# Linear attention and a sorted mixture of experts on one core: GpSimd's work beside the first block's sums of keys, five filler matmuls, and the order of the end

## The chip, the core and the metric

The kernel runs on one core of a Trainium2 chip. Its time is device time in microseconds (us) of the whole program. Five engines are named here: TensorE (PE in the profile, PEld its weight loads), VectorE (DVE), ScalarE (ACT), GpSimd (POOL) and SyncE (SP). SP only issues transfers in this kernel. ScalarE and GpSimd have DMA queues of their own. An engine executes its instructions in the order in which the program gives them. DMA transfers run beside the engines once they are issued.

## The reference, cut to what matters

The input x has 4 sequences of 2048 tokens, each of 256 numbers, all in float32. Two pre-norm layers follow each other:

```python
x = x + linear_attention(layernorm(x))     # 16 heads of 16, causal
x = x + moe(layernorm(x))                  # 8 experts, the best 2 of each token

# linear attention, per head, token after token
q, k = elu(q) + 1, elu(k) + 1
s = s + outer(k_i, v_i);  z = z + k_i
values = (q_i @ s) / (q_i . z + 1e-6);  out = values @ Wo + bo

# moe: logits over 8 experts, top 2, softmax of the two, the rest is zero
hmid = gelu(x @ w1[e] + b1[e])             # 256 -> 512
y    = hmid @ w2[e] + b2[e]                # 512 -> 256
out  = sum over the two chosen experts of weight * y
```

Two sums matter below: `z`, the running sum of keys, and the product of q and z, by which the result is divided.

## The kernel before, in words

**Attention in 16 blocks.** The 8192 tokens are cut into 16 blocks of 512. A block passes through three stages, and stage a of block s, stage b of block s−1 and stage c of block s−2 are emitted interleaved, step by step. A scheduler then orders each engine's instructions by their dependencies; SP alone keeps the order in which the program was written (`manual_schedule`, L108). `follow` (L161) forces one instruction behind another on an engine without a wait; `after` (L313) makes an instruction wait for others.

*Entering a block* (L227): VectorE takes the layernorm's statistics (L179, L182), a root is made, `xn` is written by VectorE and ScalarE (L218, L213), and GpSimd adds the output bias `bo` to x in place (L232, 128x1024), since x is used again only in stage c. For blocks up to 5 the root is one GpSimd operation, a power (L187); for later ones it is 11 small VectorE operations of Newton's method (L191 to L201).

*Stage a* (L383): TensorE transposes `xn` (pt_xn, L335) and multiplies it by Wk and Wq (pp, L402). elu+1 is two ScalarE operations (L341, L342) and one of VectorE (L343). VectorE scans k along the tokens (L412, one scan for each half of the channels, called m) and multiplies z by q in one operation of 128x1024 (L418). TensorE computes v (pv, L427), to which VectorE adds its bias (L431), and transposes k (pk, L446). Then pd (L458) sums q·z by head, VectorE adds epsilon (L464) and takes the reciprocal (L465), pr (L473) spreads it over the channels again, and VectorE divides q (L478).

*Stage b* (L487): scores (sc, L508), the causal mask (L513), the state (state_ps, L548, held in a PSUM bank of its own, then S, L559) and the values (pn, L530 and L537).

*Stage c* (L585): px multiplies the values by Wo (L597) and also gives the router's logits. VectorE adds x (L601) and the logits (L602). The sum x1 goes to `out` on ScalarE's queue (L603). VectorE picks the best two experts (L617 to L629), does the second layernorm (L632), writes the weights, token number and expert into four extra columns of the row `xn2` (L638 to L648), and, with two matmuls pc (L654, L657) that count the tokens before each one, finds each token's slot in its expert's list (L660 to L678). GpSimd then scatters the block's rows to the DRAM buffer `rows` in 8 indirect DMAs (L682).

**Experts in tiles of 256 rows.** After blocks 3, 4, 6, 8, 10, 12, 14 and 16 a `plan` (L696, VectorE) gives out a round of tiles: 5, 4, 8, 8, 8, 8, 8 and 22, so that tile 49 is the first of the last round. 68 tiles are always done and 3 more only if needed. A tile j passes through three parts:

- *turned* (L834): its rows are transposed (pt_xs, L840), copied (xT, L841), and their targets and weights taken (L847 to L853)
- *hidden* (L860): 16 matmuls with w1 (ph, L868), and gelu on ScalarE (L874)
- *output* (L879): 16 matmuls with w2 (py, L885), bias and weight on VectorE (y, L890, L894), then two scatters on GpSimd that add to `out` (L899)

TensorE's order is ph of j, pt_xs of j+1, py of j−1. SP issues, in this order for each j: rows of tile j+3 (L807), w1 of j+2 (L819), w2 of j+1 (L827), b2 of j+1 (L831). A load of rows waits for every row scatter that was emitted before it (L811). While attention is still under way, tiles are emitted between its steps; the lines after L982 share them out, and HOLD (L948) leaves five tiles to be emitted beside the last block's stage c or behind it. The last block is number 15. After it only tiles remain.

Of the kernel before, what the change touches and what calls it, by code (L numbers as in the profile page):

```python
# [16 lines left out]
P = 128  # L17
HEADS = 16
HD = 16
# [5 lines left out]
def kernel(  # L25
# [131 lines left out]

    def ins_of(i):
        return getattr(i, "ins", i)

    def follow(inst, other):  # L161

        tc.add_manual_dep(
            ins_of(inst), ins_of(other).name,
            mybir.DependencyInfo(
                mybir.DependencyClass.NoSync, mybir.DependencyReason.SCHED_ONLY
            ), reason="order of issue",
        )
# [3 lines left out]
    def layernorm(src, dst, root_of=None, power=False, behind=None, first=False):  # L172
# [11 lines left out]
        nc.vector.tensor_scalar_add(rstd, mv[:, :, 1], LN_EPS)  # L184
# [41 lines left out]

    def enter(n: int):  # L227
        xt = xs.pop(n)
        xn = att.tile([P, NT, D], F32, tag="xn", bufs=2, name=f"xn_{n}")
        std = small.tile([P, NT], F32, tag="std", bufs=3, name=f"std_{n}")  # L230
        layernorm(xt, xn, std, n <= QUIET, turn if n <= QUIET else None, n == 0)
        nc.gpsimd.tensor_tensor(  # L232
            xt, xt, bo_bc.unsqueeze(1).to_broadcast([P, NT, D]), ALU.add
        )
        entered[n] = xt, xn, std
# [52 lines left out]
    state_ps = ps_s.tile([P, NCC, 2, HD], F32, tag="state", name="state_ps")  # L288
# [17 lines left out]
    AFTER = mybir.DependencyInfo(mybir.DependencyClass.Sync, mybir.DependencyReason.DATA)  # L306
# [5 lines left out]

    def after(inst, others):  # L313
        for o in others:
            tc.add_manual_dep(inst, o.name, AFTER, reason="rows written before")

# [66 lines left out]
    def stage_a(n: int):  # L383
# [34 lines left out]
        i = nc.vector.tensor_tensor(z, z, qT, ALU.mult)  # L418
        if n > 0:
            turn[:] = [i]  # L420
        vp = vpads[n % 2]
# [20 lines left out]
        for t2 in range(NT // 2):  # L442
            pk = bank([P, 2, D], "pk")
            for j in range(2):
                for m in range(NCC):
                    nc.tensor.transpose(  # L446
                        pk[:, j, ts(m, P)], kT[:, m, ts(2 * t2 + j, P)], ident
                    )
            nc.scalar.copy(k_tok[:, 2 * t2 : 2 * t2 + 2, :], pk)
        if n < QUIET:  # L450

            enter(n + 1)
# [3 lines left out]
        for m in range(NCC):  # L456
            for t in range(NT):
                nc.tensor.matmul(  # L458
                    pd[W * t : W * t + W, :], heads[:, m, :], z[:, m, ts(t, P)],
                    start=(m == 0), stop=(m == NCC - 1), skip_group_check=True,  # L460
                    tile_position=(0, W * t),
                )
        rden = small.tile([P, P], F32, tag="rden", name="rden")
# [121 lines left out]
    def stage_c(n: int):  # L585
# [30 lines left out]
        for r in range(2):  # L616
            top = small.tile([P, NT], F32, tag=f"top{r}", name="top")  # L617
            nc.vector.tensor_reduce(top, lg, AX.X, ALU.max)
            eq = small.tile([P, NT, E], F32, tag=f"eq{r}", name="eq")
            nc.vector.tensor_tensor(eq, lg, wide(top), ALU.is_equal)  # L620
            nc.vector.tensor_tensor(eq, eq, prio_b, ALU.mult)
            first = small.tile([P, NT], F32, tag=f"first{r}", name="first")
            nc.vector.tensor_reduce(first, eq, AX.X, ALU.max)
            nc.vector.tensor_tensor(sel[:, :, r, :], eq, wide(first), ALU.is_equal)
            if r == 0:
                nc.vector.scalar_tensor_tensor(
                    lg, sel[:, :, 0, :], -3.0e38, lg, ALU.mult, ALU.add
                )
            tops.append(top)  # L629
        yield  # L630
        xn2 = att.tile([P, NT, R], F32, tag="xn2", bufs=3, name=f"xn2_{n}")
        rstd = layernorm(x1, xn2[:, :, 0:D])  # L632
# [9 lines left out]
        nc.vector.tensor_scalar_add(xn2[:, :, D], token, float(n * TB))  # L642
# [11 lines left out]
        nc.tensor.matmul(  # L654
            pc[:, 0].rearrange("p m e -> p (m e)"), before, sel_f, start=True, stop=True
        )
        nc.tensor.matmul(  # L657
# [132 lines left out]
    plans = {}  # L790

    def slot_tiles(todo):
# [4 lines left out]
        def fetch_rows(j):  # L797
# [13 lines left out]
            after(i, writes + cleared)  # L811
# [48 lines left out]
        def hidden(j):  # L860
            xT, w1t, bias = (state[j][key] for key in ("xs", "w1", "bias"))
            hT = moe.tile([P, NFC, ST], F32, tag="hT", name="hT")
            for f2 in range(NFC // 2):
                ph = bank([P, 2, ST], "ph")
                for i in range(2):
                    f = 2 * f2 + i
                    for cc in range(NCC):
                        nc.tensor.matmul(  # L868
                            ph[:, i, :], w1t[:, cc, ts(f, P)], xT[:, cc, :],
                            start=(cc == 0), stop=(cc == NCC - 1),  # L870
                        )
# [7 lines left out]
        def output(j):  # L879
# [3 lines left out]
            for a in range(NS):  # L883
                for f in range(NFC):
                    nc.tensor.matmul(  # L885
# [10 lines left out]
            def store():  # L896
                mine = []
                for a in range(NS):
# [4 lines left out]
                    ))  # L903

# [20 lines left out]
        for j in range(J + 1):  # L925
# [4 lines left out]
            if j + LEAD < J:  # L930
                fetch_rows(j + LEAD)
# [4 lines left out]
            if j > 0:  # L936
                wait.append(output(j - 1))
            while len(wait) > (j < J):
                wait.pop(0)()
            if j + 1 < J:  # L940
                fetch_out(j + 1)
            if j < J:
# [5 lines left out]
    HOLD = 5  # L948
# [24 lines left out]
    for s in range(NBLK + 2):  # L973
# [18 lines left out]
        while gens:  # L992
            for it in list(gens):
# [3 lines left out]
                while ran < share and ran * order < i * share:  # L997
# [7 lines left out]
    while work.step():  # L1005
        pass
    in_order.close()
    held = nc.values_load(holding[0][0:1, 0:1], min_val=0, max_val=ROUNDS[-1])
# [49 lines left out]
```

## Time and profile before

| | |
|---|---|
| median of 3 runs | 1089.88 us (1088.99 to 1090.7) |
| profiled execution | 1089.58 us, of which the span is 1087.9 us |
| mean granted TensorE clock | 0.972 |
| TensorE busy, 0 to 35 us | 21.83 of 35 us |
| TensorE busy, 300 to 700 us | 394.97 of 400 us |
| TensorE busy, 850 to 890 us | 28.72 of 40 us, clock 0.87 |
| TensorE busy, 890 to 1060 us | 170.00 of 170 us, DMA 0.91 busy, 233 GB/s |
| last matmul ends | 1074.89 us |
| GpSimd's bias adds (L232) | 16, from 2.34 to 2.95 us each |
| row loads, issue to landing (median) | 4.1 us |
| w1 and w2 loads, issue to landing (median) | 5.3 us |
| GpSimd's row scatters, issue to landing (median) | 2.5 us |

How to read it: the span runs from the first to the last instruction of one profiled execution; the time of a run has some 1.7 us around it. "Busy" is the time in which at least one instruction of an engine runs. The clock is the share of TensorE's full speed that the chip granted it. In a timeline a row is: start in us, duration in us, engine, source line, operation, what it writes <- what it reads, sizes, how many; in brackets how long the engine had been idle and which instruction or transfer ended that. A "chain" follows the work that ended last back, step by step, to what released it.

### The profile page before, as it was taken

How to read it: one execution, taken by the hardware profiler on the slowest of the kernel's cores; microseconds unless marked ns; L12 is line 12 of the kernel's file. 1: busy time of each engine (PE TensorE's matmuls, PEld its weight loads, DVE VectorE, ACT ScalarE, POOL GpSimd, SP SyncE). 2: the span in 40 equal slices, each digit the busy share in tenths (PEclk: the TensorE clock that was granted, in tenths of full speed). 3: DMA queues.
4: the chain of work that ended last, by engine and by line, in shares of the span. 5: the costliest groups of instructions: out<-in, count | busy, mean ns of one | idle time of the engine just before them, and what ended most of it. 6: DMA issues, size and time to landing. Idle time of an engine off the chain costs nothing.

```text
span 1087.9 us, 23077 instructions
## 1 busy us (share of the span) xinstructions
PE 1027.6 (94%) x8358; PEld 812.3 (75%) x8358; DVE 765.1 (70%) x2602; ACT 382.4 (35%) x822; POOL 394.4 (36%) x308
## 2 busy tenths in 40 slices
PE   6899998999999999999999999999999879999995
PEld 3566666576777787878787877878788768888884
DVE  7768889979788778795879777996777642333331
ACT  3424443435245335252524344252522112222220
POOL 5003034034142615153353516152424544434443
PEclk9888989999999999999999999999999989999998
DMA  6001121452527382737456472827366579999983
GB/s 215 1 21 60 40 79 41 132 167 60 148 77 204 70 257 49 241 72 211 103 163 169 105 219 58 249 49 234 69 198 163 133 238 226 242 230 228 239 206 41
DMA packets 128724, 155.22 MB, mean 143 GB/s; under 512 B 9953, under 2 KB 105953, under 8 KB 128609
## 3 DMA queue, kind: packets, MB, share of 16 engines
q1 hardware_dynamic: 85680, 102.06, 29.4%
q0 software_dynamic: 25728, 34.88, 17.9%
q10 hardware_dynamic: 17200, 16.79, 4.7%
q8 instruction: 67, 1.10, 0.4%
q14 instruction: 49, 0.39, 0.1%
HBM read 108.05 MB, written 45.65 MB: 141 GB/s over the span
## 4 chain that ended last, share of the span: by engine, by line
PE 55%; DVE 22%; DMA 3%; ACT 2%; issue 1%; POOL 0%; DVEq 0%; SPq 0%; POOLq 0%
PE ph L868 17%; PE py L885 17%; PE pn L537 4%; DVE at L513 4%; PE sc L508 3%; PE pv L427 3%; PE pp L402 2%; PE pt_xs L840 2%; PE pn L530 2%; DMA out_dram<-y,to 2%; DVE st L179 2%; DVE kT L343 1%; PE px L597 1%; DVE x L601 1%; DVE z L412 1%
## 5 line engine op out<-in xcount | busy, mean ns | idle before, releaser
L899 POOL DMA_INDIRECT out_dram<-y,to x136 | 217.4, 1599 | 475.2 <-DVE y L894 242.0
L868 PE MATMUL ph<-xT,w 128*128 128x256 f32 x1088 | 253.2, 386 | 7.0 <-DMA w<-in_w_dram 7.0
L885 PE MATMUL py<-w,hT 128*128 128x256 f32 x1088 | 249.1, 382 | 0.0
L868 PEld LDWEIGHTS ph<-xT,w 128*128 128x128 f32 x1088 | 205.9, 192 | 38.4 <-issue 8.1
L885 PEld LDWEIGHTS py<-w,hT 128*128 128x128 f32 x1088 | 202.2, 190 | 34.9 <-issue 6.3
L874 ACT ACTIVATE hT<-ph,b1t 128x256 f32<-128x256 f32 x272 | 113.6, 469 | 229.7 <-PE ph L868 223.9
L513 DVE TENSOR_TENSOR at<-sc,causal 128x512 f32<-128x512 f32 x256 | 158.0, 677 | 2.2 <-PE sc L508 1.9
L682 POOL DMA_INDIRECT rows<-xn,slots x128 | 124.4, 972 | 58.6 <-issue 34.1
L841 DVE COPY xT<-pt_xs 128x512 f32<-128x512 f32 x68 | 46.8, 688 | 130.6 <-PE pt_xs L840 130.6
L890 DVE TENSOR_TENSOR y<-py,b 128x512 f32<-128x512 f32 x68 | 46.9, 690 | 84.9 <-PE py L885 84.8
L508 PE MATMUL sc<-qM,kT 32*128 32x256 f32 x1024 | 93.3, 408 | 5.8 <-DVE at L513 2.3
L508 PEld LDWEIGHTS sc<-qM,kT 32*128 32x128 f32 x1024 | 57.1, 185 | 40.3 <-issue 10.3
L537 PE MATMUL pn<-at,vpad 128*32 128x128 f32 x2048 | 74.3, 289 | 0.0
L499 ACT ACTIVATE qM<-qs,parity 128x256 f32<-128x256 f32 x128 | 56.4, 502 | 42.9 <-DVE qs L478 38.9
L427 PE MATMUL pv<-wv_sb,xnT 128*128 128x264 f32 x256 | 62.6, 397 | 2.4 <-DVE at L513 2.4
L537 PEld LDWEIGHTS pn<-at,vpad 128*32 128x32 f32 x2048 | 55.5, 115 | 8.9 <-issue 1.3
L402 PE MATMUL pp<-xnT,wk_sb 128*128 128x512 f32 x128 | 61.1, 622 | 0.7 <-ACT xnT L336 0.7
L597 PE MATMUL px<-wo_sb,vT 128*128 128x264 f32 x256 | 61.5, 395 | 0.0
L544 ACT COPY vT<-pn 128x256 f32<-128x256 f32 x64 | 23.5, 367 | 107.9 <-PE pn L537 107.9
L402 PE MATMUL pp<-xnT,wq_sb 128*128 128x512 f32 x128 | 58.8, 600 | 0.7 <-ACT kT L342 0.6
L427 PEld LDWEIGHTS pv<-wv_sb,xnT 128*128 128x128 f32 x256 | 48.1, 194 | 13.6 <-DVE at L513 3.2
L597 PEld LDWEIGHTS px<-wo_sb,vT 128*128 128x128 f32 x256 | 48.6, 195 | 8.0 <-issue 0.2
(169 smaller groups left out, 1299.9 us busy)
## 6 DMA issues: line engine op xcount, KB each, us to landing
w<-in_w_dram SPq DMA_DIRECT2D x136, 512.0 KB, 5.3
xs<-rows SPq DMA_DIRECT2D x68, 260.0 KB, 4.1
b<-in_b_dram SPq DMA_DIRECT2D x68, 128.0 KB, 5.2
out_dram<-x ACTq DMA_DIRECT2D x16, 512.0 KB, 3.1
x<-in_x_dram ACTq DMA_DIRECT2D x15, 512.0 KB, 4.1
rows<-none SPq DMA_DIRECT2D x1, 2340.0 KB, 7.7
out_dram<-y,to POOLq DMA_INDIRECT x136, 4.1
rows<-xn,slots POOLq DMA_INDIRECT x128, 2.5
```

Source lines behind the costliest of these rows:

```text
L402: nc.tensor.matmul(pp, w[:, cc, ts(m, P)], xnT[:, cc, :], start=(cc == 0), stop=(cc == NCC - 1),)
L427: nc.tensor.matmul(pv, xnT[:, cc, ts(t, P)], wv_sb[:, cc, :], start=(cc == 0), stop=(cc == NCC - 1),)
L499: nc.scalar.activation(qM[:, :, par, :], qs[:, :, ts(c, P)], AF.Copy, scale=parity[:, par : par + 1],)
L508: nc.tensor.matmul(sc[g][:, m, :, :], kT[part, m, ts(c, P)], qM[part, m, :, :], start=True, stop=True,)
L513: nc.vector.tensor_tensor(at[:, g].rearrange("p m r i -> p (m r) i"), sc[g].rearrange("p m r i -> p (m r) i"), causal.unsqueeze(1).to_broa ...
L537: nc.tensor.matmul(pn[W * g : W * g + W, m, :], vp[:, c, NG * m + g, W * par : W * par + W], at[:, g, m, par, :], start=False, stop=(par = ...
L597: nc.tensor.matmul(px, vT[:, cc, ts(t, P)], wo_sb[:, cc, :], start=(cc == 0), stop=(cc == NCC - 1),)
L682: s = ins_of(nc.gpsimd.indirect_dma_start(out=rows[:, :], out_offset=bass.IndirectOffsetOnAxis(ap=slots[:, 2 * t + k : 2 * t + k + 1], axi ...
L868: nc.tensor.matmul(ph[:, i, :], w1t[:, cc, ts(f, P)], xT[:, cc, :], start=(cc == 0), stop=(cc == NCC - 1),)
L874: nc.scalar.activation(hT[:, f, :], ph[:, i, :], AF.Gelu, bias=bias[:, f : f + 1])
L885: nc.tensor.matmul(py[:, a, :], hT[:, f, ts(a, P)], w2t[:, f, :], start=(f == 0), stop=(f == NFC - 1),)
L899: i = ins_of(nc.gpsimd.indirect_dma_start(out=out_rows, in_=yt[:, a, :], in_offset=None, compute_op=ALU.add, bounds_check=T - 1, oob_is_er ...
```

## The change

It has two parts.

*The first block.* The bias add of block 0 is taken out of `enter` and placed behind the product of q and z of block 0; block 1's add waits for the same product. Block 1's layernorm uses the Newton operations instead of GpSimd's power. In all blocks the product of z and q is done in two halves. The PSUM bank of the state is widened by 256 columns and cleared on VectorE, and in block 0 five matmuls of the identity with Wq (128x256) write into these columns; nothing reads them. They follow the last transpose of k, and pd follows them.

*The end.* In the last block the layernorm's first step behind the statistics follows the top-2 selection, and in every block the column with the token number (L642) does. The last block's pc follows the newest expert matmul emitted at that point. A row load waits only for the scatters of the blocks of its own round, and is issued behind w1, w2 and b2 instead of ahead of them. Once all rows are written, stores of y follow the last row scatter in GpSimd's order. HOLD is 2 instead of 5, and beside the last block's stage c one expert step is placed at a fixed point. The load of the last count of tiles is done a little earlier in the program.

```diff
-    def layernorm(src, dst, root_of=None, power=False, behind=None, first=False):
+    def layernorm(src, dst, root_of=None, power=False, behind=None, first=False, last=None):
...
-        nc.vector.tensor_scalar_add(rstd, mv[:, :, 1], LN_EPS)
+        i = nc.vector.tensor_scalar_add(rstd, mv[:, :, 1], LN_EPS)
+        if last is not None:
+            follow(i, last)
...
+    def with_bias(xt, n: int):
+        i = ins_of(nc.gpsimd.tensor_tensor(
+            xt, xt, bo_bc.unsqueeze(1).to_broadcast([P, NT, D]), ALU.add
+        ))
+        if n < 2:
+            after(i, [ins_of(summed_keys[0])])
...
-        layernorm(xt, xn, std, n <= QUIET, turn if n <= QUIET else None, n == 0)
-        nc.gpsimd.tensor_tensor(
-            xt, xt, bo_bc.unsqueeze(1).to_broadcast([P, NT, D]), ALU.add
-        )
+        layernorm(xt, xn, std, n <= QUIET and n != 1, turn if n <= QUIET else None, n == 0)
+        if n > 0:
+            with_bias(xt, n)
...
-        i = nc.vector.tensor_tensor(z, z, qT, ALU.mult)
+        for m in range(NCC):
+            i = nc.vector.tensor_tensor(z[:, m, :], z[:, m, :], qT[:, m, :], ALU.mult)
         if n > 0:
             turn[:] = [i]
+        else:
+            summed_keys[0] = i
+            with_bias(xt, n)
...
+        filler = None
+        if n == 0:
+            nc.vector.memset(state_bank, 0.0)
+            for _ in range(5):
+                filler = nc.tensor.matmul(
+                    state_bank[:, NCC * 2 * HD :], ident, wq_sb[:, 0, :],
+                    start=False, stop=True, skip_group_check=True,
+                )
+                follow(filler, turning)
...
+                if filler is not None:
+                    follow(i, filler)
+                    filler = None
...
-        rstd = layernorm(x1, xn2[:, :, 0:D])
+        rstd = layernorm(
+            x1, xn2[:, :, 0:D], last=selected if n == len(blocks) - 1 else None
+        )
...
-        nc.vector.tensor_scalar_add(xn2[:, :, D], token, float(n * TB))
+        follow(
+            nc.vector.tensor_scalar_add(xn2[:, :, D], token, float(n * TB)), selected
+        )
...
+        if n == len(blocks) - 1:
+            follow(i, multiplied[0])
...
-            after(i, writes + cleared)
+            after(i, writes[: 2 * NT * ROUND_ENDS[r]] + cleared)
...
+                finished = len(writes) == 2 * NT * len(blocks) and behind_rows
...
+                    if finished:
+                        tc.add_manual_dep(i, writes[-1].name, BEHIND, reason="order of issue")
...
-            if j + LEAD < J:
-                fetch_rows(j + LEAD)
             if j + LEAD - 1 < J:
                 fetch_in(j + LEAD - 1)
...
             if j + 1 < J:
                 fetch_out(j + 1)
+            if j + LEAD < J:
+                fetch_rows(j + LEAD)
...
-    HOLD = 5
+    HOLD = 2
...
-                while ran < share and ran * order < i * share:
+                if s == NBLK + 1 and i == 2:
+                    work.step()
+                while s <= NBLK and ran < share and ran * order < i * share:
                     work.step()
                     ran += 1
```

`selected` is the last operation of the top-2 selection, `multiplied[0]` the newest expert matmul, `turning` the last transpose of k, `BEHIND` an order of issue without a wait.

## The prediction

> **What bounds the kernel now.** I read the page first, then its chain of work, then the timelines of the first 60 us and of 850 to 900 us, the chain of waits of that end, the windows of granted clock, and last how the change orders each engine's instructions. The page:
> ```profile
> PE 1027.6 (94%) x8358; PEld 812.3 (75%) x8358; DVE 765.1 (70%) x2602; ACT 382.4 (35%) x822; POOL 394.4 (36%) x308
> ...
> PE 55%; DVE 22%; DMA 3%; ACT 2%; issue 1%; POOL 0%; DVEq 0%; SPq 0%; POOLq 0%
> ```
> TensorE is busy 94% of the span and carries the chain. So only TensorE's 60 us of idle time, and the time it works at a lower clock, can be won. By windows, 13 us of the idle time are the start (0 to 35), 13 the tail (1060 to 1088), 11 the stretch 850 to 890; from 890 to 1060 TensorE is busy 170.00 of 170.00. The change addresses the start and 850 to 890.
>
> The start, timeline of all engines (start, us, engine, line; in brackets idle before and who ended it):
> ```profile
> 12.47 1.87 DVE L707 TENSOR_SCALAR steps<-count 128x33 f32<-128x33 f32 x2
> 18.52 0.16 DVE L203 TENSOR_TENSOR std<-rstd,root 128x4 f32<-128x4 f32 x1 [0.81 <-POOL root L187]
> 20.02 2.36 POOL L232 TENSOR_TENSOR x<-x,bo_bc 128x1024 f32<-128x1024 f32 x1 [1.48 <-ACT xn L213]
> 20.04 3.43 DVE L412 TENSOR_TENSOR_SCAN z<-kT 128x512 f32<-128x512 f32 x1
> 24.09 1.22 DVE L412 TENSOR_TENSOR_SCAN z<-kT 128x512 f32<-128x512 f32 x1
> 27.15 1.21 DVE L418 TENSOR_TENSOR z<-z,qT 128x1024 f32<-128x1024 f32 x1
> 28.50 0.64 PE L458 MATMUL pd<-z,heads 128*32 128x128 f32 x16 [3.25 <-DVE z L418]
> 31.49 1.24 PE L473 MATMUL pr<-rden,spread 32*128 32x128 f32 x16 [0.51 <-DVE rden L465]
> 32.66 1.97 PE L335 MATMUL pt_xn<-ident,xn 128*128 128x128 f32 x8
> ```
> The same scan takes 3.43 us beside GpSimd's bias add and 1.22 us without it, and TensorE waits 3.25 us for z·q. Then TensorE is slow: the windows grant it 0.50 from 30 to 36.
>
> The end, TensorE's timeline, then the chain of waits of the same stretch:
> ```profile
> 862.06 0.41 PE L654 MATMUL pc<-sel,before 128*128 128x64 f32 x2 [3.52 <-DVE error L199]
> 862.52 5.36 PE L868 MATMUL ph<-xT,w 128*128 128x256 f32 x16
> 886.14 5.54 PE L868 MATMUL ph<-xT,w 128*128 128x256 f32 x16 [7.02 <-DMA w<-in_w_dram]
> 895.41 3.62 PE L868 MATMUL ph<-xT,w 128*128 128x256 f32 x16
> ```
> ```profile
> 875.42 2.62 DMA rows<-xn,slots
> 878.23 0.37 SPq L807
> 878.82 7.19 DMA w<-in_w_dram
> 886.00 0.14 issue
> ```
> TensorE stops twice: 3.52 us for block 15's top-k (pc), and 7.02 us for w1 of tile 43. That load needs no row of block 15: it stands on SP's queue behind the load of tile 44's rows, which waits for block 15's last row scatter (issued 875.42). After each stop a ph of 16 matmuls takes 5.4 to 5.5 us, against 3.45 from start to start warm (895.58 to 899.03 in the chain).
>
> **Part 1, the start.** Removed from VectorE's way: the bias add of block 0 at 11.88, beside which L707 (two of 33 columns) took 1.87 us, and block 1's at 20.02; GpSimd's pow of block 1, for which VectorE waits until 18.52. Added: VectorE's Newton root for block 1, 11 operations of about 0.2 us as small ones take here, 2.4 us. Of L707's time about 1 us comes back, not all: GpSimd's second memset of vpad (1.82 us) moves up from 14.66 to about 12.4, and the first one held VectorE from 9.1 to 11. So xn is done near 17.7 and kT's first half begins at 17.8 instead of 19.32; the scan takes 1.25 instead of 3.43. In the new order VectorE then has scan, kT, scan, qT, half product, vpad, qT, vpad, half product; with these rows' durations z is ready near 25.4 instead of 28.36. ScalarE's exponentials keep up, since their buffers come free with kT's second half, at 20.8 instead of 24.05.
>
> TensorE's own work (pp, pv, pk) ends at 25.25, before and after; nothing there is shortened. Then stand the five fillers: a 128x256 matmul is 0.43 us warm (eight in the 3.45 of a ph), so 2.16 us, to 27.4. They hide z completely, and pd starts at 27.4, 1.1 us earlier. The reciprocal (L465) stood behind S (L559), which waited for ScalarE's late k_tok; with both early, pr starts near 29.95 instead of 31.49: **1.5 us**. What is late next is the fillers themselves: without them pd could start at 25.5, so they cost up to 1.9 us and must earn it by the clock.
>
> [...] In the windows the granted clock is 1.00 up to 29, 0.87 in 29 to 30, 0.50 from 30 to 36, 0.72 in 36 to 37, after one gap of 3.25 us with sparse work behind it. [...] By the rows the gap was followed by six us at half clock: pr 1.24 against 0.73 later in the run, pt_xn 1.97 against 1.04 for eight warm transposes, pp 4.66 against some 3.5, together 2.6 us, which fillers may save. Gaps of 0.5 to 1 us remain between pd, state and pr, so I take somewhat over half: 1.5. **Start: 3.0 us**, from 1.0 (no clock won, a little lost) to 4.5.
>
> What moves behind: both bias adds (4.7 us of GpSimd) now run at about 25.5 to 30.2, beside vpad, L464, S, L465 and L478. Most of these read one operand from PSUM; the stretched rows above (L412, L707) have their operands in SBUF, while block 1's statistics at 12.16, beside the first add, took their usual 0.39. I take nothing, at most 0.5 us. First reader of that x is block 0's px, tens of us later. The memset of the widened state bank is one 128x320 write among VectorE's set-up, at most 0.4 us, which ends before the scan.
>
> z·q in halves applies to every block: two of about 0.64 against one 1.21 us, 0.07 us more per block, 1.1 us of VectorE over 16, but the first half's product can precede qT's second half. VectorE is the chain for 22%; I take 0.3 us, from −1 to +3.
>
> **Part 2, the middle.** Row loads now go behind w1, w2 and b2 of the same step on SP, and wait for their own round's scatters instead of every scatter emitted. GpSimd's order shifts once: block 5's add precedes block 2's eight scatters, which delays them by up to 2.4 us. Block 2's last landed at 187.2, and SP only issued the first rows at 191.05: 3.9 us of cover. If the cover were gone, tile 0 would be late by that much with other TensorE work beside it. Elsewhere rows have 9.8 us or more until the transposes that need them. Windows from 300 to 850 leave TensorE about 5 us idle in 550, so there is nothing to win: **0, within 2 us**.
>
> **Part 3, the end.** Count from the end of px, 858.55. Before: ph of tile 41 runs from 3.97 to 9.3, and ph of tile 44 starts at 37.03 (895.58). Of this TensorE lost 3.5 (pc), 1.9 (slow ph), 7.0 (w1), 2.1 (slow ph): 14.5 us.
>
> After, pc stands behind ph of 41 and the transposes of 42, work that is ready. So ph runs 0 to 3.6, pc to 4.65, py of 40 to 7.8, ph 42, transposes 43 and py 41 to 15.1, ph 43 to 18.65. Its w1 no longer waits: w1 of 43, w2 and b2 of 42 stand ahead of tile 44's rows on SP. Queued behind that load now are w1 of 44, w2 and b2 of 43, then tile 45's rows.
>
> Does the load itself wait for less? It names only its own round's scatters. But the compiled program still makes tile 44's rows wait for the eighth scatter of block 15, the last writer of the rows buffer; tile 49 is the first that needs all of them. So the stall does not go, it moves to the rows. pc's results come at 4.65 instead of 3.9; slots, tanh and x's last column follow, so scatters start near 9.5 (before 7.95). Two stores of y of 1.55 us stand ahead as before; eight scatters at 1.27 us put the last at 18.4, it lands at 21.0 (2.6), the rows are issued at 21.2 and land at 24.3 (3.1, as the load at 878.23). TensorE has been idle since 18.65: 5.7 us. Then transposes and py of 42, partly at low clock (the two slow ph lost 1.9 and 2.1), to about 30. w1 of 44, issued at 21.8, lands after 7.2 at 29.0: just in time. ph of 44 starts near 30.4 instead of 37.03: **6.6 us**, from 3 (scatters 2 us later and w1 late in the crowded DMA) to 9 (a landing of 5 us and a clock that stays up).
>
> The tail is unchanged in order: last matmul 1074.89, last store 1081.14. Between 890 and 1060 DMA is 0.91 busy, but w1 is issued some 18 us ahead and lands in 5 to 8. Other moved steps (layernorm behind top-k, token, the store's place, `held` earlier) lie in these gaps or do not alter an order: 0.
>
> **Sum.** 3.0 − 0.3 + 0 + 6.6 = 9.3. The profiled execution took 1089.58 (span 1087.9 and 1.68 around it), 0.3 below the median 1089.88. 1089.58 − 9.3 = 1080.3, which I round to **1080**.
>
> **Rivals.**
> - The end comes in full (chance 0.14): the rows of 44 do not in fact hold TensorE, because scatters finish sooner or the wait is covered. 14.5 + 3 = 17: 1072. Against: the wait in the compiled program; for: 14.5 us were measured.
> - The start brings nothing (0.18): half clock comes anyway, and fillers only cost. 1089.58 − 6.6 = 1083.
> - The change doesn't do what it says (0.14): tile 44 still waits on block 15, its scatters are later by more than I think, and w1 of 44 lands late, so TensorE stops for 10 to 12 us instead of 5.7. End 0 to 2, start 2: 1086.5.
> - Slower (0.12): the split product and the new VectorE order cost in each attention block. VectorE is 85% busy from 100 to 300 and 22% of the chain. The place is z·q to pd in blocks 1 to 15; it decides from 0.6 us per block (9.6 in all); at 1 us per block, 16 against 9.3: 1096. Against it: halves can only cost 0.07 unless a scheduler interleaves badly, and TensorE's order is the same.
> - My forecast: 0.42.
>
> **How the numbers follow.** The likeliest is 1080. The range leaves out about 2 in 10: most of the slower case and half of the full end; 1073 to 1088. A measurement tells 0.2% apart, 2.2 us. Faster by more: my forecast, full end, start empty, and half of the third rival, 0.81; within 0.2%: the other half, 0.07; slower 0.12.
>
> **What would show it.** The first scan at 1.2 to 1.3 us, pd starting at 27 to 28, clock 1.00 in 30 to 36: Part 1. pr and pp still at 1.24 and 4.66: fillers earn nothing. TensorE without a wait for w1 but with one of about 6 us for xs<-rows in the transposes after four ph: Part 3. No such wait: the full end. If VectorE's waits before pd or sc grow from 100 to 850, the slower rival. A stall at the first tile near 190, or a w1 that lands later than 29 after px's end, would make the sum wrong.

## The result, and the profile after

| kernel | median us (runs) | ratio to before, 95% | end of px to last matmul | tail behind it | end of px to end of span |
|---|---|---|---|---|---|
| before | 1090.29 (4) | | 216.3 | 13.0 | 229.3 |
| after | 1103.8 (4) | 1.0108 [1.0076, 1.0141] | 215.3 | 25.2 | 240.5 |
| after, other session (e5) | 1094.34 (20) | 1.0048 [1.0025, 1.0071] | 213.2 | 18.3 | 231.4 |

The changed kernel is slower, by 1.1% in the first session and 0.5% in a second; 1080 was forecast. In short: the start won what was forecast. Behind it TensorE lost 8 to 9 us to half clock and idle time. At the end a write that GpSimd waits for landed later, beside loads that the change lets go earlier, and the chain of stores on GpSimd finished later than before. "px" is the last block's (block 15). The three right columns are worked out from one profiled execution each: the last matmul of px, the last matmul of all, the last instruction. The profiled execution of after took 1108.0 us, its span is 1106.1, 18.2 more than before. That splits, by the start of the same instructions in both timelines, into −1.7 until block 1's transposes, +8.8 from there to px, −1.0 from px to the last matmul, and +12.2 in the tail (rounding leaves 0.1). One profile below, e16's, is of a slow execution (1095.57 us where that kernel's median is 1083.39; 238.9 from px to the end, tail 30.3), and of it only the first 30 us behind px and the blocks before them are used.

The page:
```profile
PE 1033.6 (93%) x8368; PEld 819.3 (74%) x8368; DVE 760.9 (69%) x2630; ACT 383.1 (35%) x822; POOL 395.1 (36%) x307
...
PE 59%; DVE 22%; DMA 3%; ACT 1%; issue 1%; POOL 0%; DVEq 0%; POOLq 0%
```
The page shows almost nothing: the engines' busy shares are within a point of those before. The timelines show it. The start, all engines (lines have moved: the scan is L428, the product L435, the add L239, the fillers L476, pd L489, pr L507, pt_xn L351):
```profile
18.23 1.23 DVE L428 TENSOR_TENSOR_SCAN z<-kT 128x512 f32<-128x512 f32 x1
24.09 0.68 DVE L435 TENSOR_TENSOR z<-z,qT 128x512 f32<-128x512 f32 x1
24.85 4.68 POOL L239 TENSOR_TENSOR x<-x,bo_bc 128x1024 f32<-128x1024 f32 x2 [10.49 <-DVE z L435]
25.68 2.32 PE L476 MATMUL state_ps<-wq_sb,ident 128*128 128x256 f32 x10
27.93 0.64 PE L489 MATMUL pd<-z,heads 128*32 128x128 f32 x16
30.27 0.73 PE L507 MATMUL pr<-rden,spread 32*128 32x128 f32 x16 [0.62 <-DVE rden L499]
30.93 1.09 PE L351 MATMUL pt_xn<-ident,xn 128*128 128x128 f32 x8
```
Every step is as forecast: scan 1.23, z ready at 24.8, no wait before pd, pr and pt_xn at full clock (0.73 and 1.09 instead of 1.24 and 1.97; granted clock 1.00 from 30 to 36). But z is ready before the fillers begin (25.68), so the gap of 3.25 us would be gone without them. The end, TensorE:
```profile
865.45 3.62 PE L913 MATMUL ph<-xT,w 128*128 128x256 f32 x16
...
869.34 0.33 PE L695 MATMUL pc<-sel,before 128*128 128x64 f32 x2
...
894.72 1.09 PE L885 MATMUL pt_xs<-ident,xs 128*128 128x128 f32 x4 [10.52 <-DMA xs<-rows]
895.60 5.96 PE L930 MATMUL py<-w,hT 128*128 128x256 f32 x16
```
pc no longer holds TensorE, w1 neither; after four ph comes the wait for tile 44's rows, as forecast, but of 10.52 us and not 5.7. GpSimd in the same stretch, and the landing of block 15's attention sum x1 (the row that counts issue to landing of L637):
```profile
859.37 1.57 POOL L945 DMA_INDIRECT out_dram<-y,to  x1 [0.30 <-DVE y L939]
875.57 1.56 POOL L945 DMA_INDIRECT out_dram<-y,to  x1 [14.63 <-DVE num L798]
877.43 1.55 POOL L945 DMA_INDIRECT out_dram<-y,to  x1 [0.30 <-DVE taken L773]
879.29 0.99 POOL L725 DMA_INDIRECT rows<-xn,slots  x1 [0.30 <-DVE wt L898]
...
888.32 0.96 POOL L725 DMA_INDIRECT rows<-xn,slots  x1 [0.30 <-issue]
```
```profile
DMA to landing us min/median/max: 8.6/8.6/8.6
```
Before, the same row read:
```profile
DMA to landing us min/median/max: 2.9/2.9/2.9
```
GpSimd sits idle 14.63 us ahead of the store of tile 39. The named VectorE operation is only the last to signal; the store's y was ready at 859.2. What it waits for, in the program, is x1 of every block, block 15's too: issued at 866.15, landed 8.64 us later, at 874.79, and the store starts at 875.57. On SP the loads of tile 43's w1 and tile 42's w2 and b2, which before stood behind the blocked rows until 878.8 (20.3 us after px), now go out 2.6 to 1.2 us ahead of the end of px, and x1's 512 KB share the DMA engines with them. The 3 us behind x1's issue, before and after (columns: length, then PE, PEld, DVE, ACT and POOL busy, granted clock, DMA share, GB/s):
```profile
859.08:862.08 3.00, 0.02 (x1) 0.05 (x1) 2.97 (x28) 0.00 (x0) 0.00 (x0) 1.00 0.53 179
```
```profile
866.15:869.15 3.00, 3.00 (x17) 2.62 (x16) 2.79 (x20) 0.89 (x3) 0.00 (x0) 1.00 0.94 341
```
Before, 179 GB/s for 2.9 us are the 512 KB of x1 and little else. So the row scatters begin 13.7 us after px instead of 8.0 (before) or 9.5 (forecast).

The tail, as the chain that ended last has it, and the last stores:
```profile
1078.16 21.65 DMA out_dram<-y,to
```
```profile
1073.81 7.07 PE L930 MATMUL py<-w,hT 128*128 128x256 f32 x32
```
```profile
1097.46 1.55 POOL L945 DMA_INDIRECT out_dram<-y,to  x1 [2.99 <-DMA out_dram<-y,to]
1099.32 1.55 POOL L945 DMA_INDIRECT out_dram<-y,to  x1 [0.30 <-issue]
```
TensorE ends at 1080.9, and three pairs of stores are still to go, one each 6.4 us, since each waits for the landing of the pair before.

### The profile page after: what moved, and what is told of

It is laid out like the page before. It is cut to its first block, busy times and chain, and to the rows that moved or that the text cites. A ratio compares the mean times of both kernels' runs of the same rounds, so it can differ in the third digit from the quotient of the medians.

```text
span 1106.1 us, 23089 instructions
## 1 busy us (share of the span) xinstructions
PE 1033.6 (93%) x8368; PEld 819.3 (74%) x8368; DVE 760.9 (69%) x2630; ACT 383.1 (35%) x822; POOL 395.1 (36%) x307
## 3 DMA queue, kind: packets, MB, share of 16 engines
q0 software_dynamic: 25728, 34.88, 17.5%
## 4 chain that ended last, share of the span: by engine, by line
PE 59%; DVE 22%; DMA 3%; ACT 1%; issue 1%; POOL 0%; DVEq 0%; POOLq 0%
PE py L930 18%; PE ph L913 18%; PE pn L571 4%; PE sc L542 4%; DVE at L547 4%; PE pp L418 3%; PE pv L447 3%; PE pt_xs L885 2%; PE pn L564 2%; DVE st L186 2%; DMA out_dram<-y,to 2%; PE px L631 2%; DVE kT L359 1%; DVE x L635 1%; DVE z L428 1%; PE pk L466 1%
## 5 line engine op out<-in xcount | busy, mean ns | idle before, releaser
L913 PE MATMUL ph<-xT,w 128*128 128x256 f32 x1088 | 249.6, 383 | 0.0
L542 PE MATMUL sc<-qM,kT 32*128 32x256 f32 x1024 | 96.6, 416 | 4.8 <-DVE xT L886 2.2
L542 PEld LDWEIGHTS sc<-qM,kT 32*128 32x128 f32 x1024 | 59.8, 188 | 39.3 <-issue 10.1
L186 DVE BATCH_NORM_STATS2 st<-x 128x6 f32<-128x256 f32 x128 | 53.5, 434 | 1.6 <-DMA x<-in_x_dram 1.6
```

Source lines behind the costliest of these rows:

```text
L186: i = nc.vector.bn_stats(st[:, t, :], src[:, t, :])
L542: nc.tensor.matmul(sc[g][:, m, :, :], kT[part, m, ts(c, P)], qM[part, m, :, :], start=True, stop=True,)
L913: multiplied[0] = nc.tensor.matmul(ph[:, i, :], w1t[:, cc, ts(f, P)], xT[:, cc, :], start=(cc == 0), stop=(cc == NCC - 1),)
```

## The experiments

All ratios are to the kernel before, in the same session. Runs marked * fell in two sessions in which the kernel before took 1193 us (e1 to e4) and 1190 us (e17); their medians are compared only within a session. Each of the three right columns is from one execution. e7 and e12 leave out work, so their results are not the reference's; they serve only to tell causes apart.

| run | median us | ratio, 95% | px to last matmul | tail | px to end |
|---|---|---|---|---|---|
| e1* stores: x1 of own round | 1188.65 | 0.9932 [0.9908, 0.9956] | 209.4 | 23.7 | 233.1 |
| e16 the same | 1083.39 | 0.9936 [0.9913, 0.9960] | | | |
| e2* rows free of block 15 | 1195.89 | 1.0008 [0.9982, 1.0034] | 205.5 | 18.9 | 224.4 |
| e3* both | 1180.85 | 0.9857 [0.9809, 0.9906] | 206.2 | 18.2 | 224.4 |
| e10 both | 1082.8 | 0.9920 [0.9900, 0.9940] | 201.8 | 25.0 | 226.8 |
| e11 both, start undone | 1082.94 | 0.9934 [0.9900, 0.9969] | 201.8 | 24.8 | 226.6 |
| e14 before, both waits | 1080.23 | 0.9918 [0.9898, 0.9939] | 208.4 | 17.0 | 225.4 |
| e4* start part alone | 1189.94 | 0.9977 [0.9960, 0.9995] | 215.8 | 12.7 | 228.5 |
| e9 start part alone | 1091.34 | 0.9995 [0.9970, 1.0021] | 216.7 | 13.2 | 229.9 |
| e15 start, product whole | 1088.19 | 0.9986 [0.9970, 1.0002] | 217.3 | 13.2 | 230.5 |
| e6 end part alone | 1092.33 | 1.0032 [1.0013, 1.0051] | 213.0 | 18.1 | 231.1 |
| e7 half loads | 1089.5 | 0.9994 [0.9973, 1.0016] | 213.3 | 17.0 | 230.3 |
| e8 rows first | 1096.75 | 1.0060 [1.0042, 1.0078] | 211.4 | 23.3 | 234.6 |
| e12 one store per tile | 1087.92 | 0.9978 [0.9949, 1.0007] | 213.0 | 8.4 | 221.4 |
| e13 scatters spread | 1078.4 | 0.9890 [0.9867, 0.9913] | 201.8 | 18.6 | 220.4 |
| e17* the same, product whole | 1164.66 | 0.9806 [0.9777, 0.9836] | 201.8 | 18.6 | 220.4 |

**The two waits at the end.** In e1 and e16 a store waits only for the x1 of the blocks up to its own round's last; in e2 rows of round 6 drop the dependence on block 15's scatters; e3 and e10 do both. No order changes on any engine.
```diff
-                    after(i, added[-1] + stored)
+                    for m in range(ROUND_ENDS[todo[j][0]], len(blocks)):
+                        tc.declare_no_dep(i, group=f"sum{m}", reason="rows of other blocks")
+                    after(i, added[-1] + stored[: ROUND_ENDS[todo[j][0]]])
...
+            if r == len(ROUNDS) - 2:
+                tc.declare_no_dep(i, group=f"rows{len(blocks) - 1}", reason="rows of other blocks")
             after(i, writes[: 2 * NT * ROUND_ENDS[r]] + cleared)
```


> The changed kernel, with one wait less: a store of y waits for the attention sums of the blocks of its own round only, no longer for block 15's. Orders of all engines are the same. My theory (in the changed kernel the loads freed on SP delay block 15's sum to 8.6 us, the store of tile 39 waits for it in front of the row scatters, and the whole chain of stores starts 5.7 us late): scatters of block 15 start about 5 us earlier after px, TensorE's wait for rows falls from 10.5 to about 5.5, the chain of stores starts 5 us earlier, so 5 to 8 us less than the changed kernel, about 1096 to 1098. Rival (the stores are slow because the DMA engines are crowded, whenever they start): the tail stays near 25 us and the total falls by under 3.

The profile of e1 (px ends at 959.45 there), TensorE and GpSimd:
```profile
983.47 1.09 PE L886 MATMUL pt_xs<-ident,xs 128*128 128x128 f32 x4 [5.43 <-DMA xs<-rows]
```
```profile
968.26 0.99 POOL L726 DMA_INDIRECT rows<-xn,slots  x1 [14.51 <-DVE xn L679]
```
With the wait away, scatters begin 8.8 after px, and TensorE waits 5.43: this is the end as the prediction had it (5.7; last matmul 6.9 earlier than before, 6.6 forecast). Yet from px it takes 233.1, still 3.8 more than before, because the tail is 23.7. So with this wait away the forecast of TensorE holds, and that of the tail does not. The changed kernel itself was not run beside e1 to e4, so the gain of 5 to 8 us over it cannot be read here.

> The changed kernel with only the stores' wait for later blocks' attention sums taken away, on a chip where the kernel before takes near 1090. My theory (the freed loads delay block 15's sum to 7.5 to 9 us and so the store in front of the scatters): scatters start near 9 after px instead of 12 to 13.7, TensorE waits about 5.5 for rows instead of 8.8 to 10.5, and the end comes 3 to 5 earlier than in the changed kernel, 226 to 229 from px. Rival (scatters wait for the rows themselves): scatters at 12 or later, within 1 of the changed kernel.

Scatters again 8.8 after px and a wait of 5.27; the median falls from 1.0048 of before (e5) to 0.9936. That is more than the 3 to 5 us expected. Of the other part, 4.5 us lie between block 6's and block 15's px (517.9 against 522.4 in e5): the same wait held GpSimd in those blocks too, whose idle time ahead of its stores there falls from 303.8 to 258.9 us, and TensorE's waits before sc and pn shrink by 4.4. The 226 to 229 from px cannot be judged from this profile.

> The changed kernel, with the load of tile 44's rows (and 45 to 48) no longer waiting for block 15's scatters. Orders are the same. My theory (the chain of stores of y is what ends last): TensorE's wait of 10.5 us goes, its last matmul comes some 12 us earlier, the tail behind it grows by about as much, and the total stays within 3 us of the changed kernel, near 1103. Rival (TensorE still sets the end): 10 to 12 us less, 1092.

Here my theory fell: TensorE's wait went, and the end came at 224.4, not later than with both waits away. But the scatters also began at 8.9: x1 was not delayed here (the store that waits for it starts 4.3 after px), so the run does not separate the two. The loads went out 12 to 7 us ahead of the end of px in this run, and the DMA engines were busy 0.52 of the 3 us behind x1's issue, as before and unlike the 0.94 of after and e5. That fits the account of x1's delay.

> Both waits taken away together. My theory: stores start 5 us earlier as in the first of these kernels and TensorE does not wait at all; the total is that of the first one, within 2 us (about 1096), with a tail of over 25 us. Rival (TensorE sets the end): 14 us or more below the changed kernel, 1088 or less.

The end is that of e2, 224.4, 8.7 us earlier than e1's 233.1: "within 2 us of the first" is a miss, and so is the tail of over 25 (18.2).

> The changed kernel with both waits taken away (rows of tiles 44 to 48 on block 15's scatters; stores on the attention sums of later rounds). My theory: no wait of TensorE over 2 us behind px, its last matmul near 206 after px (216 before), but a tail of 17 to 20, so 224 to 226 to the end of the span against 229 before and 231 to 240 of the changed kernel: 2 to 6 below before. Rival (TensorE sets the end): tail 13, 219 from px, 8 to 11 below before.

In the session near 1090 TensorE has no wait of over 1.5 us behind px and ends at 201.8: all 14.5 us that the prediction had counted as lost are won. The end of the span moves by 2.5 us only, from 229.3 to 226.8; the tail takes the other 12 (25.0 against 13.0). Where the gain went is thus shown. And e16, with a TensorE wait of 5.3, has a ratio within the interval of e10. In the session at 1193 the same two kernels, e1 and e3, lie 7.8 us apart in the median. So what that wait costs stays open.

> As the one before, and with the start part undone as well: only the end of the change, with both waits taken away. My theory: from px 224 to 226 as well; the start as before; the median 3 to 6 below the kernel before, and within 2 of the kernel with both waits away and the start part in it. Rival (the start part adds its 2 to 3): 2 to 3 slower than that one.

As expected without the start part, 226.6 and a median of 1082.94: the start part adds nothing that these runs can tell.

> The kernel before with the two waits alone changed (rows of a round wait for its blocks' scatters only, stores for the attention sums of their round's blocks only); no order is changed. My theory (most of the gain of the kernel with both waits away lies in these waits): TensorE no longer waits for w1 behind px, but still 3.5 for the top-2; from px 224 to 227; 3 to 8 below before. Rival (they help only together with the new order): within 2 of before.

The kernel before with these two waits alone reaches 0.9918, the same as e10. So neither the change's orders nor its start are needed for e10's gain; of the change e14 has only the wait of row loads for their own round. 4.8 us of e14's gain lie between block 6's and block 15's px, 3.9 behind px.

**The chain of stores.** e7 halves the loads of w1 and w2 from tile 46 on, e12 leaves out the second store of a tile from 46 on, e8 puts rows in front again (as before), e13 moves the scatters: two behind each of four pairs of stores.
```diff
-                for a in range(NS):
+                for a in range(NS if j < 46 else 1):
```
```diff
                 added.append(mine)
+                for _ in range(2):
+                    if late:
+                        tc.add_manual_dep(
+                            laid[0](*late.pop(0)), mine[-1].name, BEHIND, reason="order of issue"
+                        )
```


> The changed kernel, which from tile 46 on loads only half of w1 and of w2 and uses that half twice (so the result of these tiles is not the reference's); TensorE's work and all orders are the same, the traffic of a tile falls from 1.4 to about 0.9 MB. My theory's second half (a pair of stores takes 7 to 9 us because its landing shares the DMA engines with the loads): pairs of stores fall to 6.4 to 6.7 us from the tile where loads are halved, the chain catches up with TensorE, and the tail falls from 25 to 13 to 15. Rival (the pairs are slow by themselves, or through GpSimd): periods stay at 7.5 to 8.3 and the tail at 23 to 25.

The second half of my theory fell. From tile 46 to 62 a pair takes 7.32 us with half the loads and 7.36 in e5 with all of them; the tail is 17.0 against 18.3. After the last load a pair takes 6.4. So the pairs are not lengthened in proportion to the traffic (more on this below e13).

> The changed kernel which from tile 46 on leaves out the second of the two stores of y of each tile (half of the rows of these tiles are missing in the result); all other work stays. My theory (the stores form a chain of pairs, each waiting for the landing of the pair before, which takes 6.4 us at least and 7.3 to 7.6 beside the loads, so that it never catches up with TensorE's 7.35): with one store a step takes 4.6 to 6, the chain catches up within ten tiles, and the tail falls from 18 to 25 to about 11; the last matmul stays at 213 to 215 from px, so 224 to 226 to the end. Rival (the tail is DMA traffic that must drain anyway): the tail falls by no more than 3.

This run tells that it is the chain: the rival, traffic that must drain anyway, allowed 3 us, and the tail falls by 9.9 against e5 (by 1.3 in e7, with a third of a tile's traffic gone). Two of its stores, that of tile 66 and the last:
```profile
1079.73 1.56 POOL L945 DMA_INDIRECT out_dram<-y,to  x1 [5.36 <-DVE y L939]
1084.31 1.55 POOL L945 DMA_INDIRECT out_dram<-y,to  x1 [3.02 <-DMA out_dram<-y,to]
```
A step is short enough here that stores wait for y again (5.36 idle, ended by VectorE), from tile 52 on; the tail is 8.4 instead of 18.3, with the last matmul where it was (213.0).

> The changed kernel with rows loaded ahead of w1, w2 and b2 again, as before; all else as changed. My theory (the freed loads are what lets TensorE run on and what crowds the stores): w1 of tile 43 waits behind tile 44's rows again, so TensorE waits 8 to 10 us for it, block 15's sum lands in about 3 us, scatters start near 8.5 to 9 after px, the pairs of stores return to 7.3 us and the tail to 13: 229 to 232 from px to the end, near before. Rival (the tail comes from the store's place or from the waits, not from the order of the loads): the tail stays at 20 or more.

A miss: x1 took 7.4 us here too, scatters began at 12.5, the tail was 23.3. With rows in front the load that stands still is tile 45's, and two sets of loads still go out together when block 14's scatters have landed, 6.6 us before px ends. The order on SP alone does not decide. That it is where a tile's loads are emitted among the blocks is argued, not tested.

> The kernel with both waits away, in which block 15's eight row scatters no longer stand in one piece ahead of the store of tile 40: two of them follow each of the four pairs of stores of tiles 39 to 42. Orders of the other engines are the same. My theory (the chain of stores sets the end, and it starts behind 10 us of scatters): the store of tile 40 starts 10 to 14 after the end of px instead of 19, TensorE's last matmul stays near 202 after px, the tail falls from 25 to 13 to 18, so 215 to 220 from px, 7 to 11 below the kernel with both waits away. Rival (the chain is slowed by the crowded DMA engines whenever it starts, up to the limit of the y buffers): 224 to 227 as before, tail 22 to 25.

The lowest median of all, 1078.4, though its interval overlaps those of e10 and e14. The store of tile 40 starts at 11.4 instead of 19.3, and the last pair at
```profile
1068.35 1.55 POOL L958 DMA_INDIRECT out_dram<-y,to  x1 [3.05 <-DMA out_dram<-y,to]
```
211.7 after px against 218.2 in e10. TensorE's last matmul is the same 201.8. So 6.5 of the 7.9 us won in the chain's start arrive at its end; 220.4 is just outside the 215 to 220 expected. The tail of 18.6 is still above 13: the chain does not catch up.

Why it does not is only half explained. The table gives the chain's lag: from the end of a tile's last py to the start of its first store, in us.

| tile | before | after | e5 | e7 | e10 | e13 | e14 |
|---|---|---|---|---|---|---|---|
| 42 | 1.4 | 8.0 | 8.2 | 8.7 | 13.9 | 5.0 | 6.8 |
| 48 | 1.4 | 15.4 | 10.1 | 8.7 | 18.0 | 10.0 | 7.0 |
| 54 | 1.4 | 17.5 | 9.6 | 8.4 | 17.8 | 10.2 | 7.1 |
| 60 | 1.4 | 17.9 | 10.3 | 9.4 | 17.9 | 10.3 | 8.3 |

Before, from tile 42 to 66 each first store waits for y and not for a landing, beside the same loads; tile 50's:
```profile
955.74 1.54 POOL L899 DMA_INDIRECT out_dram<-y,to  x1 [3.96 <-DVE y L894]
```
So a pair can take less than 7.35 us beside full loads. In a chain that has fallen behind a pair takes 7.35 us or more on average: the lag grows until it settles, and then the chain keeps TensorE's period, with half of the loads too (e7). The settled lags of e10 and e13, near 17.7 and 10.2, lie about one period of TensorE apart, and the tails of after and e5 differ by nearly as much (6.9). What holds a late chain at that pace stays open: the loads, let go once per tile, are a candidate that no run tests.

> The kernel with both waits away and the row scatters spread, with the product of z and q whole again in every block. My theory (the split costs 1 to 2 us of TensorE's idle time in blocks 1 to 6 and some half-clock time): idle time between block 0's and block 2's px 3.6 instead of 5.0, the end as in the spread kernel (218 to 221 from px), the median 1 to 4 us below the spread kernel's, 1075 to 1077 where the kernel before takes 1090. Rival (the split costs nothing here): within 1 us of the spread kernel.

It fell in the session with 1190; the end is e13's to 0.1 us. TensorE's idle time between block 0's and block 2's px is 8.8 there, where 3.6 was expected (10.7 to 11.8 in e1 to e4, which have the split). Its median cannot be set beside e13's, so whether the split costs in this kernel stays open.

**The start and the middle.** e4 and e9 take the start part alone, e6 the end part alone, e15 the start part with the product whole.
```diff
-        for m in range(NCC):
-            i = nc.vector.tensor_tensor(z[:, m, :], z[:, m, :], qT[:, m, :], ALU.mult)
+        i = nc.vector.tensor_tensor(z, z, qT, ALU.mult)
```


> The kernel before with the start part of the change alone (bias adds behind the products, Newton root for block 1, product in halves, fillers); the end as before. My theory (the start gains 1.8 us by block 1, and the middle's loss is where the half-clock stretches fall, not work added): 1088 to 1096, the difference to before explained by half-clock time between 40 and 340 us to within 1.5 us. Rival (the split product and VectorE's new order cost in every block): 1094 to 1097 with idle time of TensorE growing in blocks 2 to 6 even where the clock is full.

A gain of 0.2% in a session in which TensorE also waited 28.8 us before pn and 17.9 before the state for nothing in the records. So e9:

> The kernel before with the start part alone, on a chip where the kernel before takes near 1090. My theory (the start wins 2 to 3 us until block 1's transposes; behind it TensorE waits some 1 to 2 us more in blocks 1 to 6 and the half-clock stretches fall elsewhere, for better or worse): block 1's transposes 2 to 3 us earlier, the end as before (229 us from px), the median within 2 us of before. Rival (the start's gain stays): 2.5 to 4 less than before. Second rival (the start part is what made the change slow): 4 or more above before.

From the first transposes to block 1's it takes 22.5 us, before 25.0; the end is as before, and so is the median. The gain does not last. The table gives TensorE's idle time between block 0's and block 2's px, its time at half clock between block 1's transposes and block 15's px (from the clock records), and the length of the latter stretch:

| | idle, blocks 0 to 2 | at half clock | stretch |
|---|---|---|---|
| before | 3.7 | 38.0 | 822.1 |
| after | 5.0 | 51.2 | 830.9 |
| after, e5 | 5.0 | 51.2 | 829.9 |
| e9 | 5.0 | 44.4 | 825.8 |
| e15 | 3.6 | 34.1 | 818.8 |
| e6 | 3.7 | 32.4 | 819.8 |

After against before: 13.2 us more at half clock are 6.6 us of work, with 2.6 more of idle time in all; together 9.2, where 8.8 are to be explained. Both profiles of the changed kernel have the same 51.2. One window (columns as above), before:
```profile
235.00:340.00 105.00, 101.21 (x937) 76.90 (x939) 92.90 (x368) 42.61 (x89) 29.79 (x24) 1.00 0.46 135
```
and after:
```profile
235.00:340.00 105.00, 98.49 (x890) 74.33 (x889) 88.01 (x322) 41.60 (x86) 30.02 (x24) 0.93 0.39 110
```


> The start part alone, without the split of the product: one product of 128x1024 in each block, all else of the start part as it is. My theory (what is lost behind block 1 is the split's and VectorE's new order, 1 to 2 us of idle time, and the rest where half-clock stretches fall): idle time between block 0's and block 2's px falls from 5.0 to about 3.7, as before; block 1's transposes 1.5 to 2.5 earlier than before; the median 0 to 3 below before. Rival (the earlier start itself shifts the gaps into half-clock windows): idle stays at 5.0 and half-clock time between blocks 0 and 6 at 30 to 40 us; the median within 1.5 of the start part with the split.

With the product whole the idle time is 3.6 again: the split, with the VectorE order that it brings, is what costs 1.4 us of it. The median, 0.9986 [0.9970, 1.0002], hardly differs from e9's 0.9995; half-clock time falls differently from one kernel to the next (32.4 to 51.2 in the table).

> The changed kernel with its start part undone: bias adds, power for block 1, whole product and no fillers as before; the end as changed. My theory: the end costs 4 to 11 us by itself (233 to 241 us from px to the end of the span, before 229), the middle is as before within 3 us: 4 to 11 above before. Rival (the start part is what costs): within 2 us of before.

The end alone costs 0.3%, less than the 4 us expected at least, where the whole change costs 0.5% (the intervals overlap) and the start alone nothing (e9). So by the medians the loss is mostly the end's. And e5, the changed kernel again:

> The changed kernel itself once more, so that others are compared with it on one chip. My theory: from the end of px to the end of the span 236 to 241 us against 229 before, of which the tail behind the last matmul is 23 to 25 (13 before). If the loads freed on SP do not fall on block 15's sum here, the scatters start near 9 after px, TensorE waits about 5.5 us for rows, and it is near 233. Between block 1 and block 15 the difference to before is within 2 us of half of the difference in half-clock time. Rival: the middle is slower by 6 us or more in every run, by work.

x1 landed in 7.0 us, scatters began at 12.1, TensorE waited 8.8. The 236 to 241 from px and the tail of 23 to 25 did not come again: 231.4 and 18.3. Of the 7.1 us that this execution's span is longer than before, the middle makes 7.8 and the part behind px 2.1, less 2.8 won at the start. Its 20 runs spread from 1087.5 to 1108.1, the first four of after from 1095.6 to 1108.0.

## Why the prediction was wrong

- **Part 1, the start: right.** 3.0 us forecast. The first pp of block 1 ends at 36.6 instead of 39.3 (2.7). z, fillers, pd and pr came within 0.6 us of the times given, and the clock stayed up (1.00 from 30 to 36, 0.50 before). What the fillers did for it is not shown: z came early enough without them, and no run leaves them out; they took 2.3 us. So no run tells whether the 1.5 us forecast for the clock came from the fillers or from z being early.
- **Part 2, the middle, "0, within 2 us": wrong in both profiles** (+8.8, in e5 +7.8), by more time at half clock and by idle time, 1.4 us of which the split brings. The prediction had no term for where the half clock falls behind the start. With the end undone the loss is about as large as what the start wins: e9 is even with before although it wins 2.5 at the start.
- **Part 3, the scatters "near 9.5": wrong.** The stores ahead of them were taken "as before". The step that failed is that the freed loads were counted only as a gain: beside them x1 takes 8.6 us instead of 2.9 (7.0 in e5), and the store in front of the scatters waits for x1. Without that wait (e1) 5.43 was measured where 5.7 was forecast.
- **"The tail is unchanged": wrong, and the largest term of the first profile.** It was put at nothing. With 13 us of tail 1.0 to 3.1 would have been won from px; it cost 5.3 to 12.2 more. The chain of stores starts behind the scatters; once late, its pairs take TensorE's 7.35 us each or more as long as there are loads, so it does not catch up. Before, TensorE's wait of 7.0 us for w1 had let it catch up by tile 42 (lag 1.4); with that wait gone and the scatters as early as before (e14) the lag is 6.8 and the tail 17.0. The prediction looked at the order of stores and the load on DMA, not at who waits for whose landing.
- The rival "doesn't do what it says" named the late scatters and TensorE's wait of 10 to 12 us (10.52), and the 0 to 2 us left of the gain (1.0 until the last matmul), but with no loss behind it; the slower rival named the split, which is at most a small part.

## What to carry to other kernels

Before a transfer is let go earlier, write down which transfers it will run beside and who waits for their landing: here 1.2 MB of weights, let go 23 us early, went with a 512 KB write three times as long, and through it held another queue. When the bounding engine is to be sped up, give each serial chain that follows it a sum of its own, with its start and its step: a chain that falls behind and then keeps the engine's own period gives nothing back until the end. A gain of 2 us at the start of a kernel whose clock moves is only kept if the runs show it.

## What the runs showed of the hardware

- Until the last matmul, the stretches with a granted clock of 0.50 lasted 3.41, 6.83 or 10.24 us in the profile of before, and in that of after also 13.65 us, once (from 886.7, beside the wait of 10.52 us for tile 44's rows). Between 40 and 340 us they made up 34.1 us before, where TensorE's longest idle gap was 1.76 us.
- A 512 KB write took 2.9 us where the DMA engines were busy 0.53 of the 3 us behind its issue (before), and 8.6 us (after) and 7.0 us (e5) where they were busy 0.94.
- A pair of accumulating stores took 6.4 to 6.5 us in a late chain with no loads beside it (after, from 1071.7; the DMA engines were 0.35 to 0.38 busy) and 6.5 to 9.4 beside loads (after, from 900 to 1059); half of the loads left the mean of a late chain at TensorE's period (7.32 in e7 against 7.36 in e5).
- In two of the sessions the kernel before took 9% longer (1190 and 1193). In one of them TensorE waited 46.7 us in all before pn and the state for nothing that the records show (e4).
